# Smaller rooms for the lists of a two-expert layer, and one preparing product fewer

## The chip, the cores and the metric

The kernel runs on one core of one Trainium2 chip. The metric is the device time of one execution in microseconds, as the median of the runs; a profiled execution gives the trace that all views below come from.

## The reference

One layer of a graph attention network, and behind it a mixture of experts, for N = 3327 rows of 256 values, each with a residual. In short:

```python
x = x + gnn(layernorm(x), adj, W, a, gamma, beta)
x = x + ffn(layernorm(x), gate_w, gate_b, w1, w2, w3)

def gnn(x, adj, W, a, gamma, beta):          # 4 heads of 64
    h = (x @ W).reshape(n, 4, 64)
    e_row = leaky_relu(einsum('nhd,d->nh', h, a1 + a2), 0.2)
    attn = softmax(where(adj > 0, e_row[:, :, None], -9e15))
    h_prime = einsum('nhm,mhd->nhd', attn, h)
    return layernorm(h_prime) * gamma + beta

def ffn(x, gate_w, gate_b, w1, w2, w3):      # 16 experts, hidden 512
    probs = softmax(x @ gate_w + gate_b)
    top_probs, top_idx = top_k(probs, 2)     # normed to a sum of 1
    hidden = silu(x @ w1[e]) * (x @ w2[e])   # for every expert e
    return sum over the two chosen experts of top_prob * (hidden @ w3[e])
```

The inputs are drawn from a fixed seed, so how many rows choose which expert is fixed too.

## The kernel before

**Aggregation.** The rows are padded to 26 tiles of 128 and taken in seven groups of 4, 4, 4, 4, 3, 4 and 3 tiles. For each group the kernel goes over seven blocks of the adjacency matrix: SP loads a block (`sg`, L609), DVE makes a mask of ones and zeros of it (`mk`, L612), and TensorE (PE) multiplies it with the projected rows in two parts, high and low (`products`, L635 and L636, 26 x 26 pairs in all). Then `finish` closes the group: coefficients (c, L690 to L697), `rest` on GpSimd (POOL, L701), `scaled` (L707), `summed` (L718), the root of the spread on POOL (L472, L473, both in `roots`), the new rows (x, L743), transposes on PE (L759), logits (L767) and a turn back (L776), the two largest of 16 (L798), a product that gives each row its place in its expert's list (`places`, L821 to L825, read by `placed`, L837 to L843), one-hot matrices (L846, L853), and a product of them that adds the row numbers to the lists (`listing`, L860, added in L884).

**Lists.** The feed-forward part takes the rows by expert, in 19 lists. Lists 0 to 2 are experts 0 to 2 with the rows of the first five groups, lists 3 to 5 the same experts with the rest, and lists 6 to 18 the other thirteen experts in falling order of their counts. The constant `ROOM` gives for each list how many rows are computed; places behind the count get no weight. `take_list` gathers the rows by an indirect DMA of 128 rows a tile (L1007), turns them (L1211 for the first lists, a DMA transpose for the later ones), multiplies with w1 and w2, applies silu and product, multiplies with w3 (`down_products`, L1136, or L1132 where a tile's rows are few enough to share the array), weighs the rows (L1259 on ScalarE (ACT), L1261 on DVE) and adds them to the output by an indirect DMA (L1139).

The up products have two forms. Lists 0 to 5 use `up_products` (L1022) with `n = ROOM[i]` columns. Lists 6 to 18 use `by_sevenths`: the expert's rows are cut into two halves of `n // 2` columns, and seven products of sums of blocks (L1083, sums of weights and rows in L1055) replace eight. Their partial results are copied and added in PSUM (L1089, L1093), and some products are added to what another engine has written there. For that, `fix_banks` first runs one 128x512 product of ones into each of four PSUM banks (L1031), which the planner treats as one piece of work that follows the up products of the lists before:

```python
CHAIN.append(plan.add(PE, 0.9, (4, i, -1), UPS, fix_banks, [("pa", "fixed", r) for r in range(4)]))
```

Bank 0 takes product 1 of each pair of column blocks, bank 1 the copied product 0, bank 2 and 3 sums. Product 1 is issued with the flag that starts a group (`first=True`); the products into the other three are issued without it:

```python
p5 = product(1, [S["1"], X_["1"], p1, fixed], qq, lambda: ws(0), lambda: xs(0), True)
p2 = product(3, [cy], yy, lambda: a(0, 1), lambda: b(1, 0), False)
```

**The loop behind the lists.** If a list's count is over its room (`full = count > room`, L977), a loop runs over all rows for that list's expert and adds what was left out. It is skipped where no list is too full.

**The order.** All work is handed to a planner (`Plan`) as pieces with an engine, a cost, a rank and dependencies. It builds 340 orders with seeded random changes, replays each with its costs, keeps the one that ends first, and issues the instructions of every engine in that order. The order is fixed when the program is built. Costs of the list pieces are formulas of the room, such as

```python
plan.add(PE, 4 * (half / 1200 + 0.0025), (4, i, jp, number), after, emit, ...)
```

Of the kernel before, what the change touches and what calls it, by code (L numbers as in the profile page):

```python
# [55 lines left out]
P = 128  # L56
# [21 lines left out]
CAP = 512  # L78
# [8 lines left out]
LIST = 4096  # L87
NR = NE - EARLY

ROOM = [272, 352, 296, 88, 128, 112, 512, 512, 480, 472, 416, 408, 400, 400, 392, 392, 376, 376, 336]  # L90

PARTS = {m: 4 if m <= P // 4 else 2 if m <= P // 2 else 1 for m in range(1, P + 1)}

# [159 lines left out]
def gnn_moe(ctx: ExitStack, tc: tile.TileContext, x, adj_t, W, a, gamma, beta, gate_w, gate_b, w1, w2, w3, out):  # L253
    nc = tc.nc
# [39 lines left out]
    ones = const.tile([P, P], BF, name="ones")  # L294
# [34 lines left out]
    def constants():  # L329
        def ramp(t, pattern, start, step):  # L330
            nc.gpsimd.iota(t, pattern=pattern, base=start, channel_multiplier=step, allow_small_or_imprecise_dtypes=True)
# [15 lines left out]
        for k in range(2):  # L347
            ramp(behind[:, k * EARLY:(k + 1) * EARLY], [[LIST, EARLY]], k * NE * LIST, 0)
        for i, n in enumerate(ROOM):
            nc.gpsimd.memset(room[:, i:i + 1], float(n))  # L350
# [36 lines left out]
    PE, DVE, ACT, POOL, SP = "PE", "DVE", "ACT", "POOL", "SP"  # L387
# [61 lines left out]
    plan = Plan(SLOTS, take)  # L449
# [7 lines left out]
    def psum(key):  # L457
        return T[key]
# [449 lines left out]
    def early_lists(counted, lists):  # L908

        key = ("ph", "early")  # L910
        i = plan.add(DVE, 0.8, (1,), lists, lambda: indices(0))
        w = plan.add(PE, 0.05, (0,), [counted], lambda: tokens_so_far(key), [key])

        def again():
            nc.vector.tensor_copy(count[:, :EARLY], psum(key)[:, :EARLY])
            nc.vector.memset(tot[:, :EARLY], 0.0)

        return i, plan.add(DVE, 0.2, (1,), [w], again, [key])
# [98 lines left out]
    def row_tiles(n):  # L1017
        return [(t, min(P, n - t * P)) for t in range(-(-n // P))]
# [5 lines left out]
    FIXED = {}  # L1024
    CHAIN = []

    def fix_banks():

        for r in range(4):
            FIXED[r] = psum(("pa", "fixed", r))  # L1030
            nc.tensor.matmul(FIXED[r], ones, ones[:, None, :].to_broadcast([P, CAP // P, P]), start=True, stop=True)  # L1031

    def by_sevenths(i, n, xts, loaded, fixed, xtk, wk, hk, weights):

# [145 lines left out]
    def take_list(i, indexed, stored, weights, opened, order):  # L1180

        n = ROOM[i]
        tiles = row_tiles(n)
# [38 lines left out]
        hids = []  # L1222
        if i >= SEVEN:
            if i == SEVEN:
                CHAIN.append(plan.add(PE, 0.9, (4, i, -1), UPS, fix_banks, [("pa", "fixed", r) for r in range(4)]))
            hids = by_sevenths(i, n, xts, opened, CHAIN[0], xtk, wk, hk, weights)
        for j in range(JC if i < SEVEN else 0):
            keys = [("pa", "list", i, j, b) for b in range(2)]
# [87 lines left out]
    for g in range(NG):  # L1316
# [7 lines left out]
        if g == EARLY_GROUP:  # L1324
            i, c = early_lists(c, l)
            tables = [c]
            ready.update({k: (i, list(stored)) for k in range(EARLY)})
        if g == NG - 1:
            i, ranked, o = all_lists(c, l)
# [36 lines left out]
    order, told, UPS = [], [], []  # L1366
    for i in range(NL):
        of = i if i >= 2 * EARLY else i % EARLY
        if of not in weights:
            weights[of] = late_weights(of)  # L1370
        indexed, rows = ready[i]
        order = take_list(i, indexed, rows + spare[i if i < 2 else 5 if i == 2 else 0], of, [opened, weights[of]], order)
# [76 lines left out]
```

## Time and profile before

| | us |
|---|---|
| median of 3 runs | 518.4 (515.74 to 518.98) |
| the profiled execution, own time | 503.38 |
| its span in the trace | 501.7 |
| PE busy in it | 487.9 |
| DVE busy in it | 350.7 |
| ACT busy in it | 236.3 |
| POOL busy in it | 221.5 |

The profiled execution is 3% below the median of the runs. Times inside the trace add up to its own span. Busy times of engines overlap each other; a stretch in which one engine is busy all the time is bounded by it, and only there does shorter work of that engine shorten the whole. The aggregation runs until about 218 us, lists 0 to 5 with the finish of the last groups until about 282 us, lists 6 to 18 to the end.

### The profile page before, as it was taken

What the parts mean: (1) busy time and instruction counts of PE and PEld (TensorE: products, weight loads), DVE (VectorE), ACT (ScalarE), POOL (GpSimd) and SP (SyncE); (2) the same over time, 40 slices, a digit from 0 to 9 for tenths busy, and PEclk for the clock granted to TensorE, in tenths of its full rate; (3) what the DMA queues carried; (4) which work ended last, traced back from release to release, by engine and by line L of the source; (5) the groups of instructions that cost most, each with busy time, mean ns of one, the idle gap of its engine ahead of it and who ended that gap; (6) DMA issues with size and microseconds to landing.
All of it is one profiled execution on the core that took longest, in us unless ns stands there. A gap on an engine that the chain in (4) does not pass through costs nothing.

```text
span 501.7 us, 9593 instructions
## 1 busy us (share of the span) xinstructions
PE 487.9 (97%) x3239; PEld 443.0 (88%) x3240; DVE 350.7 (70%) x1035; ACT 236.3 (47%) x637; POOL 221.5 (44%) x240
## 2 busy tenths in 40 slices
PE   8999999999999999899999999999999999999993
PEld 5789999999999999887778888989998899988982
DVE  7978564976949799859773679667558777777330
ACT  3561054446264742275422367655555565454541
POOL 6320021122121330575347867658765564554253
PEclk9999999999999999999999999999999999999998
DMA  8942979898778999275239967988979878761133
GB/s 267 353 180 77 322 248 303 247 303 268 234 248 250 392 372 277 80 244 157 78 55 298 332 138 135 205 113 209 225 132 173 212 190 189 172 177 22 22 42 40
DMA packets 85704, 100.07 MB, mean 199 GB/s; under 512 B 27150, under 2 KB 59154, under 8 KB 85652
## 3 DMA queue, kind: packets, MB, share of 16 engines
q1 hardware_dynamic: 74612, 85.42, 54.6%
q0 software_dynamic: 10768, 13.75, 16.9%
q8 instruction: 26, 0.43, 0.3%
q10 hardware_dynamic: 272, 0.26, 0.2%
q14 instruction: 26, 0.21, 0.1%
HBM read 81.55 MB, written 13.75 MB: 190 GB/s over the span
## 4 chain that ended last, share of the span: by engine, by line
PE 82%; DVE 7%; DMA 4%; issue 3%; POOL 1%; ACT 1%; POOLq 1%; SPq 0%; DVEq 0%; ACTq 0%
PE ph L1136 17%; PE pa L1083 15%; PE pa L635 13%; PE pa L636 12%; PE pt L1083 11%; PE pa L1022 6%; PE ph L529 3%; DMA sg<-in_adj_t 2%; DVE mk L612 1%; PE pt L759 1%; DMA x<-in_x 1%; PE ph L1132 1%; PE ph L767 1%; PE ph L860 1%; DMA out<-y,out_index 1%
## 5 line engine op out<-in xcount | busy, mean ns | idle before, releaser
L635 PE MATMUL pa<-hi,mk 128*128 128x258 f32 x676 | 167.4, 289 | 0.0
L636 PE MATMUL pa<-lo,mk 128*128 128x256 f32 x676 | 163.1, 281 | 0.0
L1139 POOL DMA_INDIRECT out<-y,out_index x61 | 98.4, 1613 | 88.5 <-ACT y L1259 63.2
L635 PEld LDWEIGHTS pa<-hi,mk 128*128 128x128 f32 x676 | 127.7, 189 | 1.2 <-issue 1.2
L636 PEld LDWEIGHTS pa<-lo,mk 128*128 128x128 f32 x676 | 127.5, 189 | 0.1
L1136 PE MATMUL ph<-w3e,hid 128*128 128x256 f32 (+5 forms) x400 | 91.4, 380 | 0.0
L1136 PEld LDWEIGHTS ph<-w3e,hid 128*128 128x128 f32 (+5 forms) x400 | 73.9, 187 | 10.4 <-issue 0.2
L1007 POOL DMA_INDIRECT x<-normed,index x61 | 66.4, 1089 | 26.9 <-issue 18.0
L612 DVE TENSOR_SCALAR mk<-sg 128x2048 fp32r<-128x2048 f32 (+2 forms) x49 | 54.1, 1104 | 26.0 <-PE pa L636 23.7
L701 POOL TENSOR_TENSOR hp<-csum,c 128x512 f32<-128x512 f32 (+1 forms) x14 | 16.4, 1192 | 73.3 <-DVE c L697 65.5
L1083 PE MATMUL pt<-xt,w12e 128*128 128x256 f32 (+8 forms) x208 | 45.8, 345 | 0.1
L1115 ACT ACTIVATE s<-pa 128x256 f32<-128x256 f32 (+8 forms) x78 | 27.0, 346 | 37.2 <-PE pa L1083 35.5
L1259 ACT ACTIVATE y<-ph,weight 128x256 f32<-128x256 f32 (+4 forms) x50 | 23.6, 472 | 42.6 <-PE ph L1136 39.1
L1083 PEld LDWEIGHTS pt<-xt,w12e 128*128 128x128 f32 x208 | 36.2, 190 | 4.3 <-PE ph L1136 2.1
L1118 DVE TENSOR_TENSOR hid<-s,pa 128x256 f32<-128x256 f32 (+8 forms) x78 | 29.0, 372 | 11.0 <-ACT s L1115 9.9
L1093 DVE TENSOR_TENSOR pa<-pt,qs 128x512 f32<-128x512 f32 (+8 forms) x26 | 15.7, 605 | 25.3 <-PE pt L1083 24.1
L1089 ACT COPY pa<-pt 128x512 f32<-128x512 f32 (+8 forms) x52 | 25.0, 498 | 13.7 <-PE pt L1083 10.5
L1093 DVE TENSOR_TENSOR c<-pt,qs 128x512 f32<-128x512 f32 (+8 forms) x26 | 15.5, 596 | 20.9 <-ACT pa L1089 20.8
L529 PE MATMUL ph<-w_sb,xnt 128*128 128x260 f32 x104 | 26.5, 392 | 0.7 <-DVE lo L535 0.7
L1022 PE MATMUL pa<-xt,w12e 128*128 128x352 f32 (+3 forms) x128 | 26.4, 358 | 0.0
L1022 PEld LDWEIGHTS pa<-xt,w12e 128*128 128x128 f32 x128 | 19.2, 191 | 5.0 <-issue 0.6
L715 ACT ACTIVATE agg<-agg,c 128x64 f32<-128x64 f32 x76 | 18.9, 335 | 9.5 <-DVE c L697 5.2
(213 smaller groups left out, 827.1 us busy)
## 6 DMA issues: line engine op xcount, KB each, us to landing
sg<-in_adj_t SPq DMA_DIRECT2D x25, 1024.0 KB, 5.0
sg<-in_adj_t SPq DMA_DIRECT2D x20, 768.0 KB, 4.5
w12e<-in_ffn_w SPq DMA_DIRECT2D x30, 512.0 KB, 4.5
w3e<-in_ffn_w SPq DMA_DIRECT2D x15, 512.0 KB, 6.8
normed<-pay SPq DMA_DIRECT2D x5, 520.0 KB, 3.0
out<-x SPq DMA_DIRECT2D x5, 512.0 KB, 3.0
sg<-in_adj_t SPq DMA_DIRECT2D x4, 576.0 KB
x<-in_x SPq DMA_DIRECT2D x4, 512.0 KB, 5.4
```

Source lines behind the costliest of these rows:

```text
L529: nc.tensor.matmul(ph[:, :H + D], T["xnt", g, t][:, k, :], w_sb[:, k, :], start=(k == 0), stop=(k == KC - 1))
L612: nc.vector.tensor_scalar(T[mk][:, :m, :n * P], T[sk][:, :m, :n * P], 0.0, None, op0=ALU.is_gt)
L635: nc.tensor.matmul(pa[:, :D + 2], lhs, HI[mg][:, i, H:], start=first, stop=False)
L636: nc.tensor.matmul(pa[:, :D], lhs, LO[mg][:, i, H:], start=False, stop=left[g, t] == 0)
L1007: return nc.gpsimd.indirect_dma_start(out=xe[:, t, :], out_offset=None, in_=normed[:limit], in_offset=at_rows(idx, t), bounds_check=limit ...
L1022: nc.tensor.matmul(p[:, :n], wt[:, k, j * P:(j + 1) * P], xt[:, k, :n], start=(k == 0), stop=(k == KC - 1))
L1083: nc.tensor.matmul(psum(key)[:, w * (CAP // 2):w * (CAP // 2) + half], lhs()[:, w, jp], rhs(), start=first and w == 0, stop=True, skip_gro ...
L1093: return plan.add(DVE, 0.16 + 1.02e-3 * n, (1, i, jp), after, lambda: nc.vector.tensor_tensor(dst(), both(psum(xx)), T[qs][:, :, :half], o ...
L1115: nc.scalar.activation(T[gk][:, t * half:(t + 1) * half], part(0), AF.Silu)
L1118: nc.vector.tensor_mul(T[hk][:, 2 * jp + j, t * half:(t + 1) * half], T[gk][:, t * half:(t + 1) * half], part(1))
L1136: nc.tensor.matmul(py[:m, :D], hid[:, j, t * P:t * P + m], w3e[:, j, :], start=(j == 0), stop=(j == JC - 1))
L1139: i = nc.gpsimd.indirect_dma_start(out=out, out_offset=at_rows(idx, t, m), in_=y[:m], in_offset=None, bounds_check=NP - 1, oob_is_err=Fals ...
```

## The change

The rooms of eleven lists are cut to the next even number at or above what the lists hold; the other eight are as before. The product of ones into bank 0 is left out, though the bank is still taken from the pool at the same place, and the planner is given 0.65 instead of 0.9 as the cost of the three that are left. Since the planner reads rooms and costs, the order that it chooses may differ anywhere.

```diff
-ROOM = [272, 352, 296, 88, 128, 112, 512, 512, 480, 472, 416, 408, 400, 400, 392, 392, 376, 376, 336]
+ROOM = [264, 352, 296, 88, 122, 112, 512, 506, 474, 472, 414, 404, 398, 394, 388, 388, 376, 372, 336]
...
         for r in range(4):
             FIXED[r] = psum(("pa", "fixed", r))
-            nc.tensor.matmul(FIXED[r], ones, ones[:, None, :].to_broadcast([P, CAP // P, P]), start=True, stop=True)
+            if r:
+                nc.tensor.matmul(FIXED[r], ones, ones[:, None, :].to_broadcast([P, CAP // P, P]), start=True, stop=True)
...
             if i == SEVEN:
-                CHAIN.append(plan.add(PE, 0.9, (4, i, -1), UPS, fix_banks, [("pa", "fixed", r) for r in range(4)]))
+                CHAIN.append(plan.add(PE, 0.65, (4, i, -1), UPS, fix_banks, [("pa", "fixed", r) for r in range(4)]))
```

The instructions of the changed program stand one line lower than these from L1032 on; lines are given as in the kernel before.

## The prediction

> **What bounds the kernel.** I read the page's head first, then the busy time by stretch, PE's waits, the chain that ended last, and the timeline at the place where the aggregation hands over to the lists.
>
> ```profile
> span 501.7 us, 9593 instructions
> PE 487.9 (97%) x3239; PEld 443.0 (88%) x3240; DVE 350.7 (70%) x1035; ACT 236.3 (47%) x637; POOL 221.5 (44%) x240
> PE 82%; DVE 7%; DMA 4%; issue 3%; POOL 1%; ACT 1%; POOLq 1%; SPq 0%; DVEq 0%; ACTq 0%
> ```
>
> TensorE (PE) is busy 97% of the span and is 82% of the chain. Where is the rest? The busy time by stretch says (length, PE busy, PEld, DVE, ACT, POOL, clock, DMA share, GB/s):
>
> ```profile
> 150.00:200.00 50.00, 50.00 (x451) 49.29 (x450) 45.04 (x168) 24.31 (x85) 12.30 (x14) 1.00 0.97 323
> 210.00:220.00 10.00, 8.24 (x75) 7.02 (x73) 2.64 (x16) 5.79 (x20) 7.48 (x10) 1.00 0.37 111
> 350.00:450.00 100.00, 100.00 (x566) 91.69 (x565) 72.08 (x169) 54.02 (x119) 60.03 (x42) 1.00 0.82 184
> 489.00:502.00 13.00, 5.07 (x24) 3.80 (x22) 0.61 (x2) 1.71 (x4) 4.59 (x3) 0.88 0.33 38
> ```
>
> The list stage (350 to 450) has no idle PE at all: what a product there loses in length comes off the end. The tail (489 to 502) is one list's last rows. The only hole of any size in between is at 210 to 220, 1.76 us, and PE's waits name it:
>
> ```profile
> PE pt L759 <- DVE x L743: 1.6, 1, 1.6
> ```
>
> PE stands in order, and this transpose of group 5's new rows waits for DVE. The timeline of POOL and PE shows why DVE is late (start, length):
>
> ```profile
> 207.27 1.51 POOL L1007 DMA_INDIRECT x<-normed,index  x1 [4.72 <-issue]
> 209.08 1.43 POOL L1007 DMA_INDIRECT x<-normed,index  x1 [0.30 <-issue]
> 210.59 0.20 POOL L472 TENSOR_SCALAR rs_hp<-spread_hp 128x4 f32<-128x4 f32 x1
> 210.87 1.04 POOL L473 TENSOR_TENSOR rs_hp<-rs_hp,neg_half 128x4 f32<-128x4 f32 x1
> ```
>
> ```profile
> 212.49 0.85 PE L759 MATMUL pt<-ident,x 128*128 128x128 f32 x4 [1.56 <-DVE x L743]
> ```
>
> Two gathers of list 0 stand ahead of the root that group 5 needs. So this stretch depends on the order of instructions.
>
> [...] The trace agrees (a 128x256 matmul lasts 379 ns in its row but starts 216 ns after the last one), so I cost products by their pitch in the chain. [...] Bank 0 of the four prepared ones takes product 1, issued with the flag, so its preparation is not needed[...]. [...] All counts of before are multiples of four[...]. [...] two L707 on DVE took 2.45 us beside L701 on POOL, the next two 0.75.
>
> **The change, part by part.** The pitch comes from the chain:
>
> ```profile
> 270.75 3.57 PE pa L1022 x32
> 276.16 3.56 PE pa L1022 x32
> 279.72 0.86 PE pa L1031 x4
> 302.14 2.59 PE pa L1083 x12
> 448.70 1.27 PE pa L1083 x8
> ```
>
> *Columns of the product lists.* At 256 columns a record of L1083 costs 2.59/12 = 0.2158 us, at 188 columns 1.27/8 = 0.1588: 0.0570 us over 68 columns, 0.84 ns per column and record. The 13 lists have 728 records, 56 each. The halves shrink: list 7 256 to 253, 8 240 to 237, 10 208 to 207, 11 204 to 202, 12 200 to 199, 13 200 to 197, 14 and 15 196 to 194, 17 188 to 186; together 3+3+1+2+1+3+2+2+2 = 19 columns. 19 x 56 x 0.84 ns = 0.89 us, all on PE where it has no idle time.
>
> *Lists 0 and 4.* List 0: 16 products of two records, 8 columns less: 32 x 8 x 0.84 ns = 0.22 us. List 4, 128 to 122: the two L1022 lines above are lists of 128 and of 112 columns and cost the same, 0.111 us a record[...]. So nothing.
>
> *The product left out.* 0.86/4 = 0.215 us off PE, in a stretch (250 to 282) with 0.25 us of idle. Its weight load is hidden under the one before. Product 1 of list 6 now is the first write to that bank; it still waits for the chain of the other three, so no new wait.
>
> *Down products, rows, transfers.* L1136 streams 256 columns of w3 whatever the rows: nothing. All gathers still fetch 128 places and no tile disappears, so the same POOL and SP instructions; ACT and DVE save a few columns (L1115 lasts 383 ns at 256 and 337 at 200 columns, 0.8 ns a column), in the shade of PE.
>
> *Odd halves.* Lists 7, 8, 10, 12, 13 get 253, 237, 207, 199, 197. Below nothing is excluded: no row says that a shorter stream is charged less than its columns. Above: [...] if an odd start of the second half hurt every record by 10%, 5 x 56 x 0.18 us x 0.1 = 5 us. I take nothing, since no row speaks for such a price.
>
> Sum: 0.89 + 0.22 + 0.215 = 1.3 us less.
>
> *The order.* Cost and room feed the planner, so its choice of order changes on every engine from group 0's finish on. In the program of after, PE's order in the first 60 us and the order within most product lists stand as before; what moves is the finish of each group and the handover. There, counted in aggregation matmuls of 0.12 us after group 5's last: before, group 4's list product L860 at 30, group 5's transposes at 122, list 0's transposes at 156. After: L860 at 80, list 0's transposes at 156 and only then group 5's. POOL has four gathers, not two, ahead of group 5's root. Worked through with durations of before, from group 5's last matmul: DVE's coefficients end at 2.1 (1.2 us after the copy at 0.8), places 3.2, mask 4.1, one-hot pieces 4.5, L707 blocked by L701 until 5.0, then 5.5 us of pieces, L718, L846 and masks: free for L884 at 10.5. PE comes to L860 at 9.8 and ends it at 10.5: L884 is on time. From L884 to the first gather took 1.6 us (205.66 to 207.27): 12.1. Three gathers at 1.75, 1.75 and 1.4 us end at 17.0, and rows land some 2.8 us after (one issued until 217.32 released PE at 220.1): 19.8. PE wants them at 156 x 0.12 + 0.9 = 19.6: a stall of 0.2. The fourth gather ends at 18.8, the root at 20.2, L743's first tile at 20.9, while PE comes at 20.4: stalls of 0.5 and 0.2. Together 1 us, where before lost 1.76 in that stretch. Such a sum of some 25 terms is not better than 1 to 3 us, so I count the order as nothing, with -3 (every hole between 100 and 282 gone: 0.5 + 1.8 + 0.4 + 0.25) and +4 as its ends. In the stretch 150 to 200 DMA has a share of 0.97 and DVE is busy 45 of 50 us: a mask that comes a step later there would show directly.
>
> So 503.38 - 1.3 = 502.1 us against the profiled execution's own time, a ratio of 0.9974. The runs shown have a median of 518.4, 3% above it, and scatter by 0.6%; I scale: **517.1 us**.
>
> **The rivals.**
> *A, the forecast (0.60):* columns count, the order is a draw; 517.1, own range 515.5 to 519.
> *B (0.16), the order closes holes:* -3 - 1.3 = -4.3 us, scaled 514.0. For it: list 0's transposes give PE work where it waited. Against: POOL's four gathers ahead of the root.
> *C (0.18), slower, gathers ahead of the root:* with DVE late for L884, the four gathers, the root and group 5's transposes move together, and PE has nothing else in its order. From 1.3 us more stall than before the gain is gone. DVE behind by 4 us there (it was 5.9 us behind in before, 205.66 against the end of L860 near 199.8) gives +4 - 0.8 (1.0 us of stall instead of 1.76, above) - 1.3 = +1.9 us, scaled 520.4. At 6.5 us it would be slower by over 1%.
> *D (0.04), odd halves cost:* up to +5 - 1.3 = +3.7, 522.
> *E (0.02), a room is too small:* counted from the reference's inputs, with the padding row among experts 3 and 13, list 0 has 264 entries and nine lists fill their room exactly. One more and the loop behind the lists goes over all tokens for that expert: far over 5%. The smallest gap between second and third logit is 2e-5, so I give it little.
>
> **How the numbers follow.** About 1%, 5 us, is what a measurement of this kernel can tell from no change. A stays within; of B 0.04 passes 1%, of C 0.08, of D 0.02, E all of it, and scatter of the medians adds 0.01 on either side: faster 0.05, same 0.82, slower 0.13. The range reaches to B and past C's 520.4: 513.5 to 522.
>
> **What would show it.** Right: 728 records of L1083 whose pitch in lists 7 to 17 falls by 0.84 ns a column, three L1031, PE's busy time in the list stage 0.9 us less, its idle time unchanged. Wrong: a wait of PE at L1211 for the gather or at L759 for L743 of over 3 us (C), none (B), records of 253 columns not shorter than those of 256 (D), work after the last list's rows (E).

## The result and the profile after

The changed kernel takes 524.05 us (median of 6 runs, 522.67 to 525.53), the kernel before 517.37 beside it (6 runs): a ratio of 1.014, with an interval from 1.011 to 1.017. The forecast was 517.1 us, a ratio of 0.9974, with a range up to 522.0. So the change loses where a small gain was expected. All ratios in this document are those on record, with their 95% intervals; the quotient of the two medians can differ from them by up to 0.0014.

On the occasion of the later experiments the kernel before took 505 us instead of 517; times and ratios are therefore compared only with the kernel before of the same occasion. The changed kernel ran again later (label a0) and had 512.17 against 504.77: 1.0136, the same ratio. Below I read this second profile beside a second one of the kernel before (label c0). It is from another occasion, on which the kernel before took the same 505 us. In the first profile of after PE is busy for only 1.69 of the 4 us from 275 to 279, DVE and ACT hardly at all, and the clock is 0.84 of full speed between 265 and 282 us; in the second PE is busy all through both stretches at a clock of 1.00, at the same ratio, so this isn't the cause.

The page of the changed kernel, second profile (span, busy time, packets, the software queue, the scatter's group):

```profile
span 511.0 us, 9577 instructions
PE 491.2 (96%) x3238; PEld 444.9 (87%) x3239; DVE 351.6 (69%) x1035; ACT 236.0 (46%) x637; POOL 224.2 (44%) x240
DMA packets 87736, 100.09 MB, mean 196 GB/s; under 512 B 29182, under 2 KB 61186, under 8 KB 87684
q0 software_dynamic: 12800, 13.77, 17.9%
L1140 POOL DMA_INDIRECT out<-y,out_index x61 | 101.4, 1663 | 87.8 <-ACT y L1260 42.8
```

The same lines of the page of before that had not been shown:

```profile
DMA packets 85704, 100.07 MB, mean 199 GB/s; under 512 B 27150, under 2 KB 59154, under 8 KB 85652
q0 software_dynamic: 10768, 13.75, 16.9%
L1139 POOL DMA_INDIRECT out<-y,out_index x61 | 98.4, 1613 | 88.5 <-ACT y L1259 63.2
```

The forecast said that the transfers stay as they are. They don't: 2032 packets more, all of them on POOL's own queue (q0), all under 512 B, for hardly any more bytes (0.02 MB). The number of scatters is the same, 61.

Where does PE lose? The busy time by stretch of the changed kernel (length, PE, PEld, DVE, ACT, POOL, clock, DMA share, GB/s):

```profile
150.00:200.00 50.00, 49.80 (x446) 48.89 (x446) 44.05 (x165) 25.79 (x88) 10.95 (x14) 1.00 0.95 319
210.00:220.00 10.00, 9.76 (x80) 9.32 (x79) 6.26 (x27) 4.62 (x16) 7.53 (x8) 1.00 0.20 50
320.00:350.00 30.00, 25.68 (x123) 22.51 (x122) 14.57 (x33) 13.73 (x29) 16.73 (x14) 1.00 1.05 163
350.00:450.00 100.00, 98.92 (x551) 90.58 (x550) 71.34 (x169) 54.84 (x121) 60.99 (x42) 1.00 0.88 180
498.00:511.00 13.00, 2.17 (x11) 1.24 (x9) 0.00 (x0) 0.94 (x2) 4.55 (x3) 0.78 0.28 34
```

The same for the kernel before, in c0:

```profile
210.00:220.00 10.00, 8.43 (x78) 7.44 (x77) 2.70 (x13) 5.16 (x19) 8.13 (x10) 1.00 0.40 117
320.00:350.00 30.00, 30.00 (x148) 27.68 (x147) 19.49 (x42) 16.85 (x35) 20.20 (x15) 1.00 0.92 170
350.00:450.00 100.00, 100.00 (x565) 91.64 (x564) 72.46 (x170) 53.90 (x119) 59.45 (x43) 1.00 0.80 184
```

The hole at 210 to 220 us is closed (9.76 of 10 us busy, 8.43 before), and from 150 to 200 us PE is busy nearly all the time (49.80 of 50 us). The list stage, where before had no idle PE at all, lacks 4.32 us in 320 to 350 and 1.08 in 350 to 450. Where exactly can be read from an instruction that no list leaves out, the activation of the product lists (L1115 before, L1116 after, 104 of them on ACT). Its start in the changed kernel, less the start of the same one in the kernel before: -0.22 us at the 1st, -0.45 at the 21st, +2.50 at the 25th, +4.55 at the 29th, +6.99 at the 41st, +6.05 at the 49th, +5.62 at the 101st; at the end of the span +8.7. So there are four places: two near 335 and 345 us, which cost 5.0 us together, one near 378, and the tail, which costs 3.1 us. Of the 2.2 us that come in near the 41st, 0.9 are gone again by the 49th; run e2 below, which has the old work in the new order, has the same rise and return, so that part belongs to the order, and about 1.2 us stay. From the 49th on the difference falls slowly; that is the gain of the columns.

PE's longest waits in that part of the changed kernel are both for ACT (total, times, longest):

```profile
PE pt L1084 <- ACT pa L1090: 2.9, 2, 1.8
PE ph L1137 <- ACT y L1260: 2.5, 2, 2.2
```

The second is the thread to pull. PE waits for ACT to weigh rows (L1260); what does ACT wait for? The timelines of POOL, ACT and PE of the changed kernel around 335 us (start, length, idle before and releaser):

```profile
316.51 3.32 POOL L1140 DMA_INDIRECT out<-y,out_index  x1 [2.90 <-DMA out<-y,out_index]
...
330.82 1.63 POOL L1140 DMA_INDIRECT out<-y,out_index  x1 [5.66 <-DMA out<-y,out_index]
```

```profile
334.83 0.47 ACT L1260 ACTIVATE y<-ph,weight 128x256 f32<-128x256 f32 x1 [3.72 <-DMA out<-y,out_index]
```

```profile
335.36 1.99 PE L1137 MATMUL ph<-w3e,hid 128*122 128x256 f32 x8 [2.20 <-ACT y L1260]
```

Read backwards: PE has no free PSUM bank until ACT weighs, ACT has no free `y` buffer until a scatter lands, POOL's scatter of the next list waits for all scatters of the list before (`[w] + order` in `take_list`), and the scatter at 316.51 is the one of list 4, whose 122 rows are new. On POOL it lasts 3.32 us, where the mean of all is 1.66, and its last row's packet ends 13.7 us after its start, shortly before 330.82. In c0 the same two scatters stand 7.99 us apart, and PE doesn't wait:

```profile
316.61 1.58 POOL L1139 DMA_INDIRECT out<-y,out_index  x1 [3.20 <-DMA out<-y,out_index]
...
324.60 1.55 POOL L1139 DMA_INDIRECT out<-y,out_index  x1 [0.65 <-DMA out<-y,out_index]
```

The wait of PE for the copy L1090 at 345 us leads to the same place: in ACT's order that copy stands behind another weighing, which had no free `y` buffer.

```profile
344.52 0.47 ACT L1260 ACTIVATE y<-ph,weight 122x256 f32<-122x256 f32 x1 [2.73 <-DMA out<-y,out_index]
```

### The profile page after: what moved, and what is told of

Same layout as the page of the kernel before. It is cut to its first block, busy times and chain, and to the rows that moved or that the text cites. A ratio compares the mean times of both kernels' runs of the same rounds, so it can differ in the third digit from the quotient of the medians.

```text
span 523.1 us, 9577 instructions
## 1 busy us (share of the span) xinstructions
PE 497.0 (95%) x3238; PEld 448.0 (86%) x3239; DVE 351.4 (67%) x1035; ACT 235.8 (45%) x637; POOL 225.3 (43%) x240
## 5 line engine op out<-in xcount | busy, mean ns | idle before, releaser
L1137 PE MATMUL ph<-w3e,hid 128*128 128x256 f32 (+8 forms) x400 | 94.4, 386 | 3.1 <-ACT y L1260 3.1
L1137 PEld LDWEIGHTS ph<-w3e,hid 128*128 128x128 f32 (+8 forms) x400 | 74.7, 190 | 15.5 <-ACT y L1260 3.9
L1007 POOL DMA_INDIRECT x<-normed,index x61 | 65.1, 1068 | 46.9 <-issue 13.7
L701 POOL TENSOR_TENSOR hp<-csum,c 128x512 f32<-128x512 f32 (+1 forms) x14 | 16.4, 1196 | 80.0 <-DVE c L697 68.1
L1084 PE MATMUL pt<-xt,w12e 128*128 128x194 f32 (+11 forms) x208 | 46.5, 349 | 0.2
L1116 ACT ACTIVATE s<-pa 128x194 f32<-128x194 f32 (+11 forms) x78 | 27.0, 346 | 39.3 <-PE pa L1084 31.6
L1260 ACT ACTIVATE y<-ph,weight 128x256 f32<-128x256 f32 (+7 forms) x50 | 23.7, 473 | 43.8 <-PE ph L1137 29.4
L1119 DVE TENSOR_TENSOR hid<-s,pa 128x194 f32<-128x194 f32 (+11 forms) x78 | 28.8, 370 | 12.4 <-ACT s L1116 9.1
L1094 DVE TENSOR_TENSOR pa<-pt,qs 128x388 f32<-128x388 f32 (+11 forms) x26 | 15.6, 601 | 29.4 <-PE pt L1084 28.1
L1090 ACT COPY pa<-pt 128x388 f32<-128x388 f32 (+11 forms) x52 | 24.9, 495 | 20.9 <-PE pt L1084 14.9
L1094 DVE TENSOR_TENSOR c<-pt,qs 128x388 f32<-128x388 f32 (+11 forms) x26 | 15.4, 593 | 22.0 <-ACT pa L1090 18.9
L1084 PE MATMUL pa<-xsum,w12e 128*128 128x194 f32 (+11 forms) x104 | 23.1, 344 | 2.8 <-ACT pa L1090 2.8
```

Source lines behind the costliest of these rows:

```text
L1007: return nc.gpsimd.indirect_dma_start(out=xe[:, t, :], out_offset=None, in_=normed[:limit], in_offset=at_rows(idx, t), bounds_check=limit ...
L1084: nc.tensor.matmul(psum(key)[:, w * (CAP // 2):w * (CAP // 2) + half], lhs()[:, w, jp], rhs(), start=first and w == 0, stop=True, skip_gro ...
L1094: return plan.add(DVE, 0.16 + 1.02e-3 * n, (1, i, jp), after, lambda: nc.vector.tensor_tensor(dst(), both(psum(xx)), T[qs][:, :, :half], o ...
L1116: nc.scalar.activation(T[gk][:, t * half:(t + 1) * half], part(0), AF.Silu)
L1119: nc.vector.tensor_mul(T[hk][:, 2 * jp + j, t * half:(t + 1) * half], T[gk][:, t * half:(t + 1) * half], part(1))
L1137: nc.tensor.matmul(py[:m, :D], hid[:, j, t * P:t * P + m], w3e[:, j, :], start=(j == 0), stop=(j == JC - 1))
```

## The experiments

Where an order is held, a list `PLANNED` takes the place of the room in the planner's cost formulas, so that the order of instructions stays that of one kernel while the work changes. e6, e7, e9, e10 and e11 hold the order of before. The edits are shown in short: `PLANNED` and its places in the formulas are left out where they only hold the order. Ratios are against the kernel before of the same occasion.

**c0: the kernel before once more**, as the zero of the comparison.

> The kernel before, unchanged, for a second trace of it. Its trace so far is of an execution of 503.4 us, while its runs have a median of 517.4. Theory O (the order decides): time as the runs of before, ratio 1.00, and the trace shows 10 to 14 us of idle TensorE between 100 and 400 us that the first trace lacks, in places where every engine stops at once. If its trace again has 503 us, the views of before can be set against those of after as they stand.

Measured: 1.0000, from 0.9985 to 1.0015; span 502.2 us, without the idle time that theory O asked for.

**a0: the changed kernel once more** (on the occasion of e9, e10 and e12; its profile is the one read above).

> The changed kernel once more, beside the kernel before on the same chip as the experiments, where before takes 505 us. Theory R (the rows of three scatters go over 2, 2 and 4 DMA engines): new work in the old order gave 1.0247, the new order alone 0.9955; if they add, the changed kernel is at 1.020, 515 us, and the gates of its product lists have the two steps, about 5 to 8 us before the 25th gate and about 2 us later. Theory P (the pause of all engines at 275 to 279 us in its first profile, and the halved clock beside it, belong to it and come in every run): 1.035 to 1.04, 523 us, and the pause is in this profile too.

Measured: 1.0136 (1.0097 to 1.0174). The pause of theory P is not in this profile, and the ratio is below what both theories gave: loss and order don't simply add.

**e1 and e2: order and work taken apart.** First theory: the planner's new order costs the time. Rival: the work does. The planner's cost for the preparing products goes with the order too, 0.9 in e1 and 0.65 in e2.

```diff
 # e1: work of after, order of before
+ROOM = [264, 352, 296, 88, 122, 112, 512, 506, 474, ...]   # after
+PLANNED = [272, 352, 296, 88, 128, 112, 512, 512, 480, ...] # before, in every cost formula
 # e2: the other way round
```

> The rooms and the three products of the changed kernel, in the order of the kernel before: the planner is given the old rooms and the old cost 0.9, so ACT, DVE, POOL and SP issue the same instructions in the same order as before, with fewer columns, and PE the same without the one product. Theory O (the loss is the new order alone, the work itself saves 1.3 us): ratio to before 0.9974, 516.0 us for 517.4. Theory W (odd counts of columns or the missing product cost more than they save): ratio over 1.005, up to 1.014.

> The old rooms and all four products, in the order of the changed kernel: the planner is given the new rooms and 0.65. Theory O: the whole loss and the saved work on top, ratio to before 1.014 + 0.0026 = 1.0166, 526.0 us. Theory W: as before, ratio 1.000 within 0.003.

Measured: e1 1.0247 (1.0221 to 1.0273), e2 0.9955 (0.9935 to 0.9975). The theory of the order falls: the order gains 0.45%. All of the loss is in the work, more of it than theory W had allowed. And the packets go with the work: e1 has the changed kernel's, e2 those of before.

```profile
q0 software_dynamic: 12800, 13.77, 17.7%
```

That is e1's line for the software queue; e2 has 10768 packets. Their sizes in the trace say more: the rows of 1024 B are 6656 in both, the packets of 8 B are 2240 instead of 208. In e1 they come in three bursts, about 850, 850 and 350. During the first two the rows pass some 18 a microsecond and during the third some 30, where in the same places of c0 90 to 110 rows pass within one. The counts that are new at these places are 122 (list 4), 122 (last tile of list 7) and 116 (last tile of list 17): 2 x 61, 2 x 61, 4 x 29.

What do these counts have in common that 128 and 120 have not? An assumption, theory R: the rows of such a scatter go in equal shares to the largest number of DMA engines, at most 16, that divides their count. By that, 122 rows go over 2 engines with 61 rows each, 116 over 4 with 29, and 128, 126 and 120 over 16, 14 and 15 with 8, 9 and 8. No run up to here shows it, so it had to be measured with the indirect scatter that adds.

**m1: the scatter alone.** The kernel writes zeros to the output and then issues the scatter with the counts below, three times over, each after the landing of the one before; everything else is left out. The edit in short:

```diff
+    def add(m):
+        nc.gpsimd.indirect_dma_start(out=out, out_offset=IndirectOffsetOnAxis(ap=out_index[:m, 0:1], axis=0), in_=y[:m],
+                                     in_offset=None, bounds_check=NP - 1, oob_is_err=False, compute_op=ALU.add)
+    for m in (128, 126, 124, 122, 120, 118, 116, 113, 112, 90, 88) * 3: add(m)
```

> This kernel leaves everything of the reference out: it writes zeros to the output and then issues the disputed operation alone, the indirect scatter that adds rows of 1 KB to the output, one after the other, for 128, 126, 124, 122, 120, 118, 116, 113, 112, 90 and 88 rows, three times over; each waits for the one before. Theory R (rows go in equal shares to the largest number of DMA engines, at most 16, that divides their count): with about 0.1 us a row and engine, as in the trace of the first run, 122 and 118 rows (2 engines with 61 and 59 rows) land some 5 us later than 128 and 120 rows (16 and 15 engines with 8 rows); 124 and 116 (4 engines, 31 and 29 rows) some 2 us later; 113, a prime (1 engine) some 10 us later; 126, 112, 90 and 88 (14, 16, 15, 11 engines) like 128. Rival M (any count that isn't a multiple of 8 is slow): 126 and 90 rows are as late as 122. Rival H (the scatter isn't to blame, the odd halves of the product lists are): all counts land alike, within 0.5 us.

The timeline of POOL in its second round, in the order of the counts from 128 to 112 (start, length; in brackets the wait for the landing of the scatter before):

```profile
96.98 1.55 POOL L85 DMA_INDIRECT out<-y,out_index  x1 [2.56 <-DMA out<-y,out_index]
100.93 1.57 POOL L85 DMA_INDIRECT out<-y,out_index  x1 [2.40 <-DMA out<-y,out_index]
105.01 2.22 POOL L85 DMA_INDIRECT out<-y,out_index  x1 [2.51 <-DMA out<-y,out_index]
112.73 2.96 POOL L85 DMA_INDIRECT out<-y,out_index  x1 [5.50 <-DMA out<-y,out_index]
123.39 1.62 POOL L85 DMA_INDIRECT out<-y,out_index  x1 [7.70 <-DMA out<-y,out_index]
127.64 2.91 POOL L85 DMA_INDIRECT out<-y,out_index  x1 [2.63 <-DMA out<-y,out_index]
138.09 2.10 POOL L85 DMA_INDIRECT out<-y,out_index  x1 [7.54 <-DMA out<-y,out_index]
145.52 4.35 POOL L85 DMA_INDIRECT out<-y,out_index  x1 [5.33 <-DMA out<-y,out_index]
162.01 1.48 POOL L85 DMA_INDIRECT out<-y,out_index  x1 [12.13 <-DMA out<-y,out_index]
```

From one start to the next is what a scatter costs in all. Mean of the three rounds of one profiled execution (two for the last row, since nothing follows it), with the 8 B packets of each from the trace:

| rows | engines x rows each, by R | start to start, us | POOL's own part, us | 8 B packets |
|---|---|---|---|---|
| 128 | 16 x 8 | 4.0 | 1.6 | none |
| 126 | 14 x 9 | 4.1 | 1.6 | 18 |
| 124 | 4 x 31 | 7.5 | 2.2 | 372 |
| 122 | 2 x 61 | 10.9 | 3.0 | 854 |
| 120 | 15 x 8 | 4.1 | 1.6 | 8 |
| 118 | 2 x 59 | 10.8 | 2.9 | 826 |
| 116 | 4 x 29 | 7.2 | 2.1 | 348 |
| 113 | 1 x 113 | 16.4 | 4.4 | 1695 |
| 112 | 16 x 7 | 3.9 | 1.5 | none |
| 90 | 15 x 6 | 3.7 | 1.5 | 6 |
| 88 | 11 x 8 | 4.0 | 1.6 | 40 |

Theory R holds for every count: the time follows the rows that one engine gets, not the count and not its being a multiple of 8 (126 and 90 are fast). The small packets fit too: each is the number of engines that got no rows times the rows of one that did (14 x 61 = 854, 15 x 113 = 1695). The same product over all lists gives 144 for the kernel before and 2228 for the changed one. The rooms hold 6720 and 6668 places for 6656 rows; with one packet for each of the 64 and 12 places behind a count, every 8 B packet is accounted for: 144 + 64 = 208 and 2228 + 12 = 2240.

Do these small packets take the time, or the rows? In the round shown, the 8 B packets of the 122 rows pass between 3.55 and 6.53 us after the start, the rows between 3.54 and 10.01, each for 0.10 us. So the end is set by the rows, which stand in line: never more than 4 of their packets overlap at 122 rows and 2 at 113, but 22 or more at 128. The traces don't number the engines; that the rows sit on so few is read from the times, these overlaps and the products.

**e5: three counts mended**, all else as in the changed kernel, its order too (`PLANNED` has the changed kernel's numbers).

```diff
-ROOM = [264, 352, 296, 88, 122, 112, 512, 506, ..., 388, 388, 376, 372, 336]
+ROOM = [264, 352, 296, 88, 126, 112, 512, 510, ..., 388, 388, 376, 376, 336]
```

> The changed kernel, with its order of instructions, one product left out and all its smaller rooms, except three: list 4 gets 126 instead of 122, list 7 510 instead of 506 (its last tile 126 rows), list 17 376 instead of 372 (its last tile 120 rows). Theory R: the three scatters are spread over 14, 14 and 15 DMA engines instead of 2, 2 and 4; the whole loss goes, and order (0.9955 when it was tried alone) and columns (some 0.9 us less) are left: ratio 0.993, at most 0.998; the 2032 additional packets of 8 bytes are gone. Rival M (multiple of 8 needed): two of the three stay slow, ratio about 1.02. Rival H (odd halves): lists 7, 8, 10, 12 and 13 still have odd halves, ratio about 1.01 to 1.025.

Measured: 0.9945 (0.9923 to 0.9966). The page of e5:

```profile
span 500.5 us, 9577 instructions
PE 489.3 (98%) x3238; PEld 444.7 (89%) x3239; DVE 351.5 (70%) x1035; ACT 236.6 (47%) x637; POOL 219.8 (44%) x240
q0 software_dynamic: 10800, 13.75, 17.2%
```

And the place of the stall, in e5, with the same order of instructions:

```profile
315.45 1.60 POOL L1140 DMA_INDIRECT out<-y,out_index  x1 [2.96 <-DMA out<-y,out_index]
...
325.02 1.56 POOL L1140 DMA_INDIRECT out<-y,out_index  x1 [1.54 <-DMA out<-y,out_index]
```

List 4's scatter takes 1.60 us on POOL and list 5's starts 9.57 us after it, instead of 14.31; PE waits for no `y` any more, and of the 2032 further packets 32 are left. Four rows more in each of lists 4, 7 and 17 turn a loss of 1.4% into a gain of 0.55%. The odd halves 237, 207, 199, 197 and a new one of 255 are all in e5, so they cost nothing that shows. The pitch of the products (median from one start to the next) says the same, and for 253 columns too: in a0 216 ns at 256 columns, 213 at 253, 200 at 237, 175 at 207, 168 at 199 and 167 at 197; in c0 202.5 at 240, 176 at 208 and 169 at 200.

**e6 and e7: list 4 alone, in the kernel before.**

```diff
-ROOM = [272, 352, 296, 88, 128, 112, ...]
+ROOM = [272, 352, 296, 88, 122, 112, ...]   # e6; 126 in e7
```

> The kernel before, with its order, and one number changed: list 4 has 122 rows instead of 128. Theory R: this one scatter costs what the first run of the new work in the old order lost between the 23rd and the 25th gate of the product lists, 7 us: ratio 1.013 to 1.016. Rival H (odd halves): list 4 has no halves, ratio 1.000. Rival S (it takes several slow scatters together to hurt): under 1.004.

> The kernel before, with its order, and list 4 with 126 rows instead of 128. Theory R: 126 is 14 times 9, so 14 DMA engines take 9 rows each, nothing is late: 1.000 within 0.002. Rival M (multiple of 8 needed): as with 122 rows, 1.013 to 1.016.

Measured: e6 1.0045 (1.0028 to 1.0062), e7 1.0007 (0.9990 to 1.0024). The direction is R's, the size isn't: 2.5 us and not 7. I had taken the step in the single profile of e1 for the price of list 4 alone. This stretch swings, without a slow scatter too: e7's profiled run is 1.1 us behind c0 at the 1st activation and 4.7 at the 25th and has a span of 507.0 us, though its 20 runs have a median of 505.57, within 0.2% of before. One profile can't price a stall here.

**e9 and e10: list 17 alone, list 7 alone.**

```diff
+ROOM[17] = 372   # e9 (376 before): last tile 116 rows
+ROOM[7] = 506    # e10 (512 before): last tile 122 rows, halves of 253 columns
```

> The kernel before, with its order, and one number changed: list 17 has 372 rows, so its last tile has 116 instead of 120 (and the halves 186 instead of 188 columns). Theory R: 116 is 4 times 29, and 116 rows took 7.0 us from one scatter to the next in the kernel that only scatters, 120 rows 4.0; in the tail the last rows stand behind them and nothing is left to hide it: 3 us later, less 0.1 us for the columns: ratio 1.005 to 1.007. Rival I (only several slow scatters together hurt): 1.000.

> The kernel before, with its order, and list 7 has 506 rows: its last tile 122 rows instead of 128, its halves 253 columns instead of 256. Theory R: the second step of the new work in the old order, 1.8 us near the 51st gate, less 0.14 us for the columns: ratio 1.003 to 1.005. Rival H (an odd half hurts every product of its list): a loss spread over list 7's 56 products, at least 0.5 us there. Rival I (only several slow scatters together hurt): 1.000.

Measured: e9 1.0033 (1.0018 to 1.0047), e10 1.0028 (1.0010 to 1.0047). Both lose, 1.7 and 1.4 us, each less than its scatter lasts longer in m1 (3 and 7 us), and both a little less than expected. In the tail the chain is easy to see. The last scatters of list 17 and the first of list 18 in the kernel before (c0), then in e9:

```profile
487.61 1.61 POOL L1139 DMA_INDIRECT out<-y,out_index  x1 [0.30 <-ACT s L1115]
493.71 1.58 POOL L1139 DMA_INDIRECT out<-y,out_index  x1 [4.49 <-ACT y L1259]
```

```profile
487.96 2.08 POOL L1139 DMA_INDIRECT out<-y,out_index  x1 [0.30 <-ACT s L1115]
495.76 1.58 POOL L1139 DMA_INDIRECT out<-y,out_index  x1 [5.72 <-ACTq L1377]
```

In before, the next scatter waits for its own rows (ACT `y`); the landing of list 17 is hidden behind that. In e9 it starts 1.7 us later, after 7.80 us instead of 6.10; list 17's scatter lands 7.02 us after its start there, and the releaser that the trace infers (L1377, the end of ACT's list work) says nothing about that. In the changed kernel the trace names the landing outright:

```profile
493.24 2.10 POOL L1140 DMA_INDIRECT out<-y,out_index  x1 [0.30 <-ACT s L1116]
501.66 1.57 POOL L1140 DMA_INDIRECT out<-y,out_index  x1 [6.32 <-DMA out<-y,out_index]
```

**e11: lists 4 and 7 together.** The three alone multiply to 1.0106. But e5 and the changed kernel, 0.9945 and 1.0136, differ by a factor of 1.0192 and only in these three rooms.

> The kernel before, with its order, and two numbers changed: list 4 has 122 rows, list 7 506. Alone list 4 gave 1.0045, list 7 1.0028 and list 17 1.0033, together 1.0106; but all three with the other smaller rooms gave 1.0247 in the same order, where columns and product bring about 0.25%, so 1.7% more than the sum. Theory A (the scatters' delays add; the rest is from elsewhere, such as the other rooms): 1.007. Theory Q (the two slow scatters in a row lengthen each other's wait: what the first leaves late, the second finds): 1.015 to 1.024.

Measured: 1.0155 (1.0121 to 1.0190), where the two alone multiply to 1.0073. The size is theory Q's: slow scatters cost more together than one by one. Its mechanism, how the first would reach the second, isn't shown. e11's profiled run (509.61 us) lies below its median of 511.65. It has a step near 335 us (5.7 us from the 21st to the 25th activation, of which 0.6 come back) and one near 390 us (0.9); the single profiles of e6 and e10 have 4.1 us at the first place and 4.4 at the second, so the steps don't explain the excess. Why it is there stays open.

**e12: the mended counts, and an order of the planner's own.** `PLANNED` is left out, so costs follow the mended rooms.

> The changed kernel with list 4 at 126, list 7 at 510 and list 17 at 376 rows, and the planner working with these numbers, so with an order of its own; everything else as changed. Theory R: no slow scatter is left, the columns and the product bring 0.25%, the order is a draw between that of before (0) and that of after (-0.45%): ratio 0.991 to 0.998. Rival H (odd halves): above 1.01.

Measured: 0.9940 (0.9917 to 0.9963), 501.9 us against 504.77; the same as e5 within the interval. It is the version to keep: it beats the kernel before by 0.6% and the changed one, on the same occasion, by 2.0%.

## Why the prediction was wrong, step by step

- *Down products, rows, transfers: nothing.* **This is the step that failed.** The forecast argued from the number of instructions: "no tile disappears, so the same POOL and SP instructions". The number is the same, 61 scatters, but their cost isn't a function of the number of rows alone: taken alone in m1, list 4's goes from 4.0 to 10.9 us, list 7's last the same, list 17's from 4.1 to 7.2. In the kernel the three together cost 1.9% (1.0136 against 0.9945 in e5), some 9.6 us where the forecast had nothing. In the kernel before each tile that is not full has a count with a largest divisor of 8 to 16 (16, 96, 40, 88, 112, 32, 24, 8, 120, 80), so no row of its profile could show the price. m1, the scatter alone, is the run that shows it. On PE the step holds: eight records of L1136 last 1.89 us at 128 rows and at 112 (before, from 274.27 and from 280.42 us).
- *In the list stage it looked at PE only.* The forecast went through PE's instructions for what they save, put ACT and DVE "in the shade of PE" and what POOL and the transfers do at nothing. That held while scatters landed in time. The path from a late landing to PE is three waits long (list order on POOL, `y` buffers on ACT, PSUM banks on PE), and no part of the sum looked at how much room it had.
- *Columns, 0.84 ns each.* Right. e5 has 15 of the 19 columns: 15 x 56 x 0.84 ns = 0.71 us (lists 7 and 17 take back 4). The start of its activations against the kernel before moves from -0.87 us at the first to -1.59 at the 103rd: 0.72.
- *List 0 and the product left out, 0.22 + 0.215 us.* Right. That bank 0 can do without its product was an assumption of the forecast; the traces show only the time. The four weight loads of these products last 98 to 113 ns each and stand between 279.45 and 280.09 us in before, where PE runs products without a gap (276.00 to 280.59), so they are hidden. e5 and e2 have the same order, and e5's first activation of the product lists is 0.45 us earlier (287.57 against 288.02). Taken together the columns, list 0 and the product should be worth 1.1 us in e5 against e2; the ratios, 0.9945 and 0.9955, say 0.5, each with an interval of about 1 us on either side.
- *Odd halves, nothing.* Right, by e5 and by the pitch of each width, 253 columns included (213 ns in a0, 216 at 256).
- *The order, nothing, with -3 and +4 as ends.* The size was missed inside its ends: e2 gives -0.45%, 2.3 us. The stretch where the forecast feared a stall was improved: at 210 to 220 us PE lacks 0.24 us in e2 and 1.57 in c0. But e2's profile ends only 0.4 us before c0's (501.8 and 502.2), so most of the 2.3 us is in the runs and not in the one profile; where, stays open.
- *The rivals.* None of them was it. B (order closes holes) is half right and hidden behind the loss; C (four gathers ahead of the root) fails, since in a0 no wait of PE for L743, which needs that root, is over 0.31 us (`PE pt L759 <- DVE x L743: 0.7, 3, 0.3`). D fails with e5 and the pitch. E, far over 5% by the forecast's estimate, fails with the measured 1.4%. The forecast left 0.13 for slower, mostly for C, a wrong reason; its "At 6.5 us it would be slower by over 1%" is also a little off by its own sum, 6.5 - 0.8 - 1.3 = 4.4 us, or 0.9%.

The sum without the failed step, 0.9974, with the measured order gives about 0.993; e5, where only that step is mended, measured 0.9945.

## What to carry to other kernels

Before a size is cut to what the data needs, time each transfer of that size alone, at the old count and at the new one, as m1 does. For the scatter measured here the largest divisor up to 16 of its rows decides (4.1 us at 126 rows, 10.9 at 122); for other transfers no run here shows it. In m1 a count with a large prime factor (122, 118, 116, 113) is worse than a larger one with a good divisor (126, 120): the 15 columns that e5 saves are worth 0.72 us, and one such scatter alone lasts 3 to 12 us longer (7.2 to 16.4 instead of 4.1). Count packets by queue in both profiles: a rise at equal bytes (2032 packets, 0.02 MB) was the fingerprint here, visible on the page before any timeline. And where a step is costed at nothing because another engine covers it, follow the chain of buffers from it to that engine once, and price the cover in microseconds.

## What the runs showed of the hardware that was not expected

- An indirect scatter of 122 rows of 1 KB lasts 10.9 us from start to start, one of 126 rows 4.1; 113 rows take 16.4 (m1). POOL's own part grows too, from 1.6 us at 126 rows to 4.4 at 113.
- The scatter brings small packets of 8 B, as many as the engines that by theory R got no rows times the rows of one that did (854 at 122 rows in m1, 1695 at 113). The rows of 1024 B have their own packets, 6656 in before and after alike; at 122 rows the small ones are done 3.5 us before the last row.
- Two such scatters, 1.0045 and 1.0028 alone, give 1.0155 together in this kernel.
